# Splitting the convolution's x loads and v stores by partitions: 120 and 8, later 108 and 20, then 88 and 40

## The chip, the core and the metric

The kernel runs on one core of a Trainium2 chip. The metric is the device time of one execution in microseconds; lower is better. A profiled execution also gives the span of the program's instructions, which is a little shorter than the device time, and all positions in time below ("at 207 us") are counted from the start of that span.

## The reference, cut to what matters

Two layers, each of the form x + f(group norm of x), on x of shape 16 images × 16 channels × 256 × 256, float32:

```python
# layer 0: a circular 3x3 convolution, written in the reference with FFTs
x = x + conv3x3_circular(gn(x), L0_conv_weight)
# layer 1: a Laplace neural operator (poles and residues)
x = x + laplace(gn(x), ty, tx, poles1, poles2, residues)

def gn(v, G=8, eps=1e-5):          # per image and group of 2 channels
    ...
    return (g - mean) / sqrt(var + eps)

def laplace(...):
    alpha = fft2(x)                # steady part: alpha times a rational function, back by ifft2
    S = einsum('ikpq,oikp,xikq->oxik', residues, A, Bm)
    x1 = ifft2(einsum('biox,oxik->bkox', alpha, S)).real
    ...                            # transient part: sums over poles of exp(pole * t)
    return x1 + x2 / Nx / Ny
```

The change concerns layer 0 alone: how its input x comes into the on-chip memory and how its result, called v, goes out to DRAM.

## The kernel before, in words

The program has four stages, one after the other: the convolution (29 to 587 us), transforms of v along y and x (to about 1125 us), the mixing of channels (to about 1860 us), and the transforms back with the output. The change is in the first.

**How an image is laid out.** The 128 partitions hold 4 row groups × 2 rows × 16 channels. An image comes as two halves, tiles `xt` of 128 partitions × 18 rows × 258 floats, in a pool of five buffers. `load_x` loads a half in four parts (`PARTS`: rows 0, 4, 10, 14, 18), one DMA each from `load_part` (L132). In DRAM each partition's two neighbouring rows are one piece of 2064 bytes, so a part has 2 or 3 pieces per partition.

**The order of work.** The stage is written out by hand in a loop over `g`, 24 steps per image (L687). Its first call in each step is `conv(g)` (L292): 16 matmuls of 32 × 32 on 512 columns, four row groups side by side (they stand in the profile as 768 matmuls and 768 weight loads of L306 per image). After six steps a quarter of an image's sums is ready: ScalarE copies it out of PSUM into `pair` and `far` (L325). Two steps later `mirror` lets VectorE form the sum of the two halves (L273) and GpSimd the difference (L276). ScalarE squares both for later statistics (L284). Seven and eight steps after the copy, the two `vD<-pair` stores are issued (L335), eight per image; each piece in DRAM is 2048 bytes. `pair` has three buffers, `far` two.

**When x is loaded.** Images 0 and 1 are loaded before the loop. In image b, at steps 4, 5, 10, 11 of each half image, one part of image b + 2 is loaded. Its first reader is VectorE: `x_stats(b)` (L184) takes moments by `bn_stats` (L191), one row pair each, and at fixed steps before the image begins gathers them, spreads them by a matmul (L219), forms the variances (L229 to L239) and at the end the scaled weights `wc` (L249). The convolution of the image can't begin before `wc`.

**Queues.** All these loads and stores are issued by SyncE (SP), in program order. An instruction that waits, a store for GpSimd's difference for instance, holds up those behind it. SP uses eight completion semaphores in turn, and an issue waits until the earlier transfer on its semaphore has landed.

**Beside it.** A generator, `tables`, is advanced once per step and builds tables for the second layer: among others it loads `s_h` in five transfers (L455) at about 62, 129, 203 and 276 us, and stores `cD` in eight (L647) between 385 and 520 us. At the end of the stage the first loads of v for the next stage, `s<-vD` (L746), follow the last stores on SP.

Of the kernel before, what the change touches and what calls it, by code (L numbers as in the profile page):

```python
# [16 lines left out]
B = 16  # L17
C = 16
N = 256
P = 128  # L20
# [4 lines left out]
def conv_then_laplace_kernel(ctx: ExitStack, tc: tile.TileContext, a: dict, out: bass.AP):  # L25
# [15 lines left out]
    nc = tc.nc  # L41
    x = a["x"]
# [29 lines left out]
    vD = []  # L72
    for b in range(B // 4):
        t = dp.tile([P, C, 8 * N + 256], FP, name=f"vD{b}", tag=f"vD{b}")
# [53 lines left out]

    PARTS = 0, 4, 10, 14, 18

    def load_part(t, b, h, i, j):
        nc.sync.dma_start(  # L132
            out=t[:, i:j].rearrange("p (n r) x -> p n (r x)", r=2),
            in_=x[b][:, 8 * h + i // 2 : 8 * h + j // 2, 0 : 2 * (N + 2)],
        )

    def load_x(b, h):
        t = xp.tile([P, 18, N + 2], FP, name="xt", tag="xt")
        for i, j in zip(PARTS, PARTS[1:]):
            load_part(t, b, h, i, j)  # L140
        return t
# [129 lines left out]
    def mirror(g, b, u, pair, hi):  # L271
        both, lo = pair[:, :, :, 0], pair[:, :, :, 1]
        nc.vector.scalar_tensor_tensor(  # L273
            both, lo, 1.0, hi, ALU.mult, ALU.add, accum_out=sums[:, b, u : u + 1]
        )
        nc.gpsimd.tensor_tensor(lo, lo, hi, ALU.subtract)  # L276
        folded.extend((g + 7 + r, b, u, pair, r) for r in range(2))
        squared.append((g + 5, lambda: square(both, 4 + 2 * u, b, bias=shift2[:, b : b + 1])))
        squared.append((g + 7, lambda: square(lo, 5 + 2 * u, b)))
# [12 lines left out]
    def conv(g):  # L292


        for c in range(4):
            for r in range(4):
                at = g if r < 2 else g - 3
                if not 0 <= at < 24 * B:
                    continue
                b, u, n = at // 24, at // 6 % 4, at % 6  # L300
                phase, tap = n // 3, n % 3
                if n == 0 and c == 0:
                    acc[r] = pc.tile([P, 2, N], FP, name="ps_conv", tag="ps_conv")
                q = 8 * (u % 2) + c + phase + (r < 2)
                rows = slice(32 * r, 32 * r + 32)
                nc.tensor.matmul(  # L306
                    acc[r][32 * c : 32 * c + 32],
                    lhsT=ready[b][0][rows, phase, tap],
                    rhs=halves[b][u // 2][rows, q : q + 5 : 4, 2 - tap : 2 - tap + N],
                    start=n == 0,  # L310
                    stop=n == 5,
                )
        for r in (0, 1) if g % 6 == 5 else (2, 3) if g % 6 == 2 else ():
            at = g if r < 2 else g - 3
            if not 0 <= at < 24 * B:
                continue
            b, u = at // 24, at // 6 % 4
            if r == 0:
                pair = vp.tile([P, 2, 2, 2, N], FP, name="pair", tag="pair")
                acc["v", 0] = pair, pair[:, :, :, 1]  # L320
            elif r == 2:
                far = fp.tile([P, 2, 2, N], FP, name="far", tag="far")
                acc["v", 1] = far, far
            to = acc["v", r // 2][1]
            nc.scalar.activation(to[:, r % 2], acc[r], AF.Identity, bias=ready[b][1])  # L325
            if r == 3:
                later.append((g + 2, lambda g=g, b=b, u=u, pair=acc["v", 0][0], hi=to: mirror(g, b, u, pair, hi)))
        while later and (later[0][0] <= g or g >= 24 * B + 2):
            later.pop(0)[1]()
        while squared and (squared[0][0] <= g or g >= 24 * B + 2):  # L330
            squared.pop(0)[1]()
        while folded and (folded[0][0] <= g or g >= 24 * B + 2):
            _, b, u, pair, r = folded.pop(0)
            y = 64 * r + 16 * u
            nc.sync.dma_start(  # L335
                out=vD[b // 4][y : y + 16, :, b % 4].rearrange("(t y) c h x -> (y c) t (h x)", t=2),
                in_=pair[:, r].rearrange("p t h x -> p t (h x)"),
            )

    vs = tp.tile([P, 5, B], FP, name="vs", tag="vs")  # L340
    vrhs = tp.tile([P, 2, B, C], FP, name="vrhs", tag="vrhs")
# [345 lines left out]
    for g in range(24 * B + 3):  # L687
        conv(g)
        if g - 24 * (B - 4) in (16, 19, 22, 27, 30, 33):
            next(early, None)  # L690
        b, n = divmod(g, 24)
        if b + 2 < B and n % 12 in (4, 5, 10, 11):
            h, k = n // 12, (4, 5, 10, 11).index(n % 12)
            if k == 0:
                halves.setdefault(b + 2, []).append(
                    xp.tile([P, 18, N + 2], FP, name="xt", tag="xt")
                )
            load_part(halves[b + 2][h], b + 2, h, PARTS[k], PARTS[k + 1])
        for b, gen in at_step.get(g, ()):
            going.append([b, gen, next(gen)])  # L700
        for it in list(going):
            while it[2] is not None and g >= 24 * it[0] - it[2][0]:
                it[2][1]()
                it[2] = next(it[1], None)
            if it[2] is None:
                going.remove(it)
        run_jobs(g, slots.get(n, ()))
        next(tables, None)
# [32 lines left out]
    m, n = cols[:, 16:17], cols[:, 17:18]  # L741
# [140 lines left out]
    nsgn, first = mcol[:, 7:8], mcol[:, 8:9]  # L882
# [61 lines left out]
    for u in range(len(units) + 1):  # L944
        at = units[u] if u < len(units) else None
        if at is not None:
            now = vq
            t = lp.tile([P, 2, 4, 3, P], FP, name="t", tag="t")
# [8 lines left out]
        if last is not None:  # L957
            i, b0 = last[:2]
# [13 lines left out]
        if last is not None:  # L972
            first_slots(b0, spec, *done)
            if b0 == B - 4:
                project(i, psd)
                (nc.sync if i + 1 < C else nc.scalar).dma_start(
                    out=aD[:, 2 * i : 2 * i + 2], in_=spec.rearrange("p r f b -> p r (f b)")
# [25 lines left out]
    pair = a0.tile([P, 4, 4, 2, 16, B], FP, name="abd01", tag="abd01")  # L1003
# [420 lines left out]
    for n, (k, b0) in enumerate(units):  # L1424
# [13 lines left out]
        r = rp.tile([P, 4, 2, N], FP, name="r", tag="r")  # L1438
# [169 lines left out]
```

## Time and profile before

| | us |
|---|---|
| median of three runs | 2661.2 (2646.39 to 2662.68) |
| profiled execution, device time | 2645.82 |
| profiled execution, span | 2643.7 |
| convolution stage (29 to 587 us of the span) | 558 |
| PE busy in that stage | 507.1 |
| VectorE (DVE) busy in that stage | 409.8 |

In the profile, PE is TensorE's matmuls and PEld its weight loads, DVE is VectorE, ACT ScalarE, POOL GpSimd, and SPq the transfers that SyncE issues. A row of a tile, as `xt<-in_x`, names what is written and what is read. A wait row gives the engine and line that waited, what released it, the total, the number of times and the longest. "issue" stands where the profile shows no releaser. The page's rows with 40 digits cut the span into equal slices of 66 us and give the busy share in tenths; "share of 16 engines" means the 16 DMA engines of the core.

### The profile page before, as it was taken

The page shows a single profiled execution, that of the slowest core. Times are in us where ns is not written, and L with a number is a line of the kernel's source. Part 1 is how long each engine was busy: PE and PEld are TensorE (multiplying, and loading weights), DVE is VectorE, ACT ScalarE, POOL GpSimd, SP SyncE. Part 2 cuts the span into 40 slices and gives each one's busy share as a digit, 9 for nine tenths or more (in the row PEclk, how much of TensorE's full clock was granted, in tenths as well). Part 3 has the DMA queues.
Part 4 walks back from the last instruction along what each step waited for, and adds up shares of the span by engine and source line. Part 5 has one row for each costly group of instructions (what it writes and reads, how often), then busy time and mean ns, then how long its engine had stood idle before and what let it go on. Part 6 is the DMA issues. An engine that isn't in the chain of part 4 may idle for free.

```text
span 2643.7 us, 83901 instructions
## 1 busy us (share of the span) xinstructions
PE 2483.2 (94%) x35314; PEld 1880.4 (71%) x35314; DVE 1983.8 (75%) x3805; ACT 1450.5 (55%) x2727; POOL 1327.4 (50%) x1179
## 2 busy tenths in 40 slices
PE   5988899889999999998999999999799999999998
PEld 2444454466777777775887878888688888888887
DVE  7767778838888888888787878888266676667666
ACT  2555566575666666665666666666244444444443
POOL 1333368432333333334476746676556565665653
PEclk9999999999999999999999999999899999999999
DMA  8787778855465556545777777877988888888884
GB/s 278 267 282 271 268 244 296 287 189 186 192 255 233 193 212 241 224 189 219 225 229 223 229 228 217 236 227 230 257 284 304 286 292 277 295 290 279 294 284 172
DMA packets 313399, 653.11 MB, mean 247 GB/s; under 512 B 44566, under 2 KB 159382, under 8 KB 301120
## 3 DMA queue, kind: packets, MB, share of 16 engines
q1 hardware_dynamic: 311856, 640.55, 71.7%
q8 instruction: 278, 4.55, 0.7%
q0 software_dynamic: 896, 3.02, 0.4%
q10 hardware_dynamic: 272, 4.19, 0.4%
q14 instruction: 97, 0.79, 0.1%
HBM read 368.15 MB, written 280.36 MB: 245 GB/s over the span
## 4 chain that ended last, share of the span: by engine, by line
PE 61%; DMA 5%; DVE 4%; SPq 4%; ACT 2%; issue 1%; POOL 1%; ACTq 0%; DVEq 0%; POOLq 0%
PE ps_mix L1120 9%; PE ps_y L777 9%; PE ps_p L1361 9%; PE ps_y L785 8%; PE ps_f L1385 8%; PE ps_f L1386 8%; PE ps_x L820 5%; DMA yD<-yt 4%; PE ps_s L1032 2%; SPq L1134 2%; PE ps_h L1345 2%; PE psd L805 1%; DVE sg L1052 1%; ACT yt L1233 1%; SPq L1102 1%
## 5 line engine op out<-in xcount | busy, mean ns | idle before, releaser
L1120 PEld LDWEIGHTS ps_mix<-abd,sg 128*64 128x64 f32 x8192 | 450.6, 138 | 85.9 <-ACT yt L1233 54.1
L1120 PE MATMUL ps_mix<-abd,sg 128*64 128x128 f32 x8192 | 480.7, 276 | 32.5 <-DMA yD<-yt 17.7
L306 PE MATMUL ps_conv<-xt,wc 32*32 32x512 f32 x12288 | 453.5, 618 | 45.2 <-issue 37.2
L1325 POOL TENSOR_TENSOR u<-yk 128x512 f32<-128x512 f32 (+1 forms) x268 | 352.3, 1347 | 282.8 <-PE ps_p L1361 215.5
L306 PEld LDWEIGHTS ps_conv<-xt,wc 32*32 32x32 f32 x12288 | 254.7, 104 | 231.9 <-issue 147.7
L793 ACT ACTIVATE t<-ps_y,vmr 128x384 f32<-128x384 f32 x512 | 297.5, 581 | 162.6 <-PE ps_y L785 162.5
L1052 DVE STREAM_SHUFFLE sg<-ps_s 128x512 f32<-128x512 f32 (+1 forms) x264 | 329.3, 1316 | 0.0
L777 PE MATMUL ps_y<-tabE,vq 128*128 128x256 f32 x1024 | 313.1, 388 | 13.4 <-DVE vq L766 11.7
L276 POOL TENSOR_TENSOR pair<-pair,far 128x1024 f32<-128x1024 f32 x64 | 151.8, 2372 | 332.9 <-DVE pair L273 277.5
L785 PE MATMUL ps_y<-tabO,vq 128*128 128x256 f32 x1024 | 305.6, 380 | 0.0
L1385 PE MATMUL ps_f<-pt,inv 128*128 128x256 f32 x1008 | 300.4, 380 | 0.0
L1361 PEld LDWEIGHTS ps_p<-inv,u 128*128 128x128 f32 x2048 | 266.2, 193 | 47.3 <-issue 25.5
L1386 PE MATMUL ps_f<-hs,ey 128*128 128x256 f32 x1008 | 299.8, 379 | 0.0
L1389 DVE TENSOR_TENSOR r<-ps_f,q 128x256 f32<-128x256 f32 x256 | 107.1, 418 | 252.7 <-ACT q L1388 252.7
L1361 PE MATMUL ps_p<-inv,u 128*128 128x128 f32 x2048 | 279.3, 280 | 10.5 <-POOL u L1329 10.4
L1049 ACT ACTIVATE sg<-ps_s,mcol 128x512 f32<-128x512 f32 (+1 forms) x264 | 179.5, 690 | 184.4 <-DVE sg L1052 117.0
L777 PEld LDWEIGHTS ps_y<-tabE,vq 128*128 128x128 f32 x1024 | 189.3, 190 | 90.2 <-ACT q L833 50.3
L1388 ACT COPY q<-ps_f 128x256 f32<-128x256 f32 x256 | 95.4, 373 | 288.1 <-PE ps_f L1386 285.4
L765 POOL TENSOR_TENSOR vq<-vf 128x512 f32<-128x512 f32 x64 | 81.5, 1274 | 294.5 <-DVE vf L769 277.6
L1363 ACT COPY pt<-ps_p 128x512 f32<-128x512 f32 x256 | 150.2, 587 | 132.6 <-PE ps_p L1361 128.0
L1233 ACT COPY yt<-ps_mix 128x512 f32<-128x512 f32 x352 | 185.1, 592 | 55.3 <-DMA yD<-yt 43.3
L785 PEld LDWEIGHTS ps_y<-tabO,vq 128*128 128x128 f32 x1024 | 195.4, 191 | 26.8
(239 smaller groups left out, 4050.8 us busy)
## 6 DMA issues: line engine op xcount, KB each, us to landing
vD<-pair SPq DMA_DIRECT2D x128, 512.0 KB
yD<-yt SPq DMA_DIRECT2D x512, 128.0 KB
vl<-vD SPq DMA_DIRECT2D x128, 512.0 KB
out_y<-ol SPq DMA_DIRECT2D x128, 512.0 KB
s<-vD SPq DMA_DIRECT2D x126, 512.0 KB
aD<-spec SPq DMA_DIRECT2D x15, 4096.0 KB
yk<-yD SPq DMA_DIRECT2D x60, 1024.0 KB
xt<-in_x SPq DMA_DIRECT2D x96, 516.0 KB
```

The source lines that it names most:

```text
L306: nc.tensor.matmul(acc[r][32 * c : 32 * c + 32], lhsT=ready[b][0][rows, phase, tap], rhs=halves[b][u // 2][rows, q : q + 5 : 4, 2 - tap : ...
L777: nc.tensor.matmul(ps[:, 0:N], lhsT=vf[:, xo, 0, j], rhs=tabE[:, 0 : i + 2 : i + 1], start=True, stop=False, skip_group_check=True,)
L785: nc.tensor.matmul(ps[:, P : P + N], lhsT=vf[:, xo, 1, j], rhs=tabO[:, i : C + 1 : C - i], start=False, stop=True, skip_group_check=True,)
L793: nc.scalar.activation(t[:, xo, j].rearrange("p l n -> p (l n)"), ps[:, 0:384], AF.Copy, scale=vmr[:, 0, b0 + j, i : i + 1],)
L1049: nc.scalar.activation(to[..., k : k + 2], src[odd], AF.Copy, scale=nsgn)
L1052: nc.vector.stream_shuffle(to[..., C + k : C + k + 2], src[1 - odd], swap)
L1120: nc.tensor.matmul(ps[64 * t : 64 * t + 64, j], lhsT=sg[:, f : f + 2].rearrange("p f m -> p (f m)"), rhs=abd[jq][:, :, 2 * t + cc, 2 * jj ...
L1233: (nc.vector.tensor_copy if m >= (2 if late else 3) else nc.scalar.copy)(o, src)
L1325: nc.gpsimd.tensor_tensor(u[:, :, j].rearrange("p b (c n) -> p c b n", c=8), in0, in1, o)
L1361: nc.tensor.matmul(ps[:, at], lhsT=u[:, n], rhs=tab, start=True, stop=True)
L1385: nc.tensor.matmul(ps[:, e], lhsT=tab, rhs=pt[:, e], start=True, stop=False)
L1386: nc.tensor.matmul(ps[:, e], lhsT=ey[:, e], rhs=hs, start=False, stop=True)
```

## The change

A helper gives a cut of the 128 partitions for an image number: 120 for images below 6, 108 below 11, 88 from there on. Each part of x from image 2 on is loaded by two DMAs, one for the partitions below the cut and one for the rest. Each store of v is likewise two DMAs, with the cut of the image that is being loaded at the time (two ahead, at most 15). What is transferred, the tiles and all other instructions stay as they are.

```diff
+    def spans(b):
+
+        first = 120 if b < 6 else 108 if b < 11 else 88
+        return (0, first), (first, P)
+
     def load_part(t, b, h, i, j):
-        nc.sync.dma_start(
-            out=t[:, i:j].rearrange("p (n r) x -> p n (r x)", r=2),
-            in_=x[b][:, 8 * h + i // 2 : 8 * h + j // 2, 0 : 2 * (N + 2)],
-        )
+        for p, q in spans(b) if b > 1 else ((0, P),):
+            nc.sync.dma_start(
+                out=t[p:q, i:j].rearrange("p (n r) x -> p n (r x)", r=2),
+                in_=x[b][p:q, 8 * h + i // 2 : 8 * h + j // 2, 0 : 2 * (N + 2)],
+            )
...
             y = 64 * r + 16 * u
-            nc.sync.dma_start(
-                out=vD[b // 4][y : y + 16, :, b % 4].rearrange("(t y) c h x -> (y c) t (h x)", t=2),
-                in_=pair[:, r].rearrange("p t h x -> p t (h x)"),
-            )
+            to = vD[b // 4][y : y + 16, :, b % 4].rearrange("(t y) c h x -> (y c) t (h x)", t=2)
+            for p, q in spans(min(b + 2, B - 1)):
+                nc.sync.dma_start(out=to[p:q], in_=pair[p:q, r].rearrange("p t h x -> p t (h x)"))
```

## The prediction

> **What bounds the kernel now.** I read the page first, then the convolution by windows of one image (cut at every 768th matmul of L306, which is an image's worth), its waits, and the order of time around one image boundary, each with its lines here.
>
> ```profile
> DMA  8787778855465556545777777877988888888884
> ...
> q1 hardware_dynamic: 311856, 640.55, 71.7%
> ...
> vD<-pair SPq DMA_DIRECT2D x128, 512.0 KB
> ...
> xt<-in_x SPq DMA_DIRECT2D x96, 516.0 KB
> ```
>
> ```profile
> 387.80:422.30 34.50, 32.21 (x851) 17.23 (x845) 29.99 (x53) 23.82 (x47) 32.34 (x34) 1.00 0.92 316
> 422.30:457.80 35.50, 33.06 (x848) 17.71 (x838) 30.57 (x54) 22.62 (x45) 27.86 (x30) 0.95 0.78 271
> ...
> 535.00:560.90 25.90, 25.90 (x780) 18.15 (x785) 16.17 (x38) 17.51 (x33) 8.34 (x4) 1.00 0.45 166
> 560.90:586.80 25.90, 25.90 (x788) 19.21 (x761) 4.93 (x8) 20.16 (x34) 10.89 (x6) 1.00 0.46 166
> ```
>
> The convolution is the first eight and a half slices (29 to 587 us), and DMA is busy there at 7 to 8 tenths, nearly all of it on SP's queue q1 and most of it with stores of v and loads of x. In the windows the columns are length, busy time of PE, PEld, DVE, ACT, POOL, clock, DMA share and GB/s. Images 10 and 11 take 34.5 and 35.5 us at a DMA share of 0.92 and 0.78; images 14 and 15, with no x left to load, take 25.9 us at 0.45, with PE never idle. So PE sets the pace, but something in the images with loads costs it time.
>
> The waits of 33 to 590 us (total, times, longest), then the timelines of SP, DVE and PE around image 6:
>
> ```profile
> POOL pair L276 <- DVE pair L273: 275.3, 48, 47.3
> ...
> PE ps_conv L306 <- issue: 37.2, 26, 5.0
> ...
> DVE xst L191 <- DMA xt<-in_x: 16.4, 5, 5.4
> ```
>
> ```profile
> SPq L335 <- POOL pair L276: 202.8, 44, 8.5
> ...
> SPq L132 <- DMA s_h<-hD: 6.6, 6, 1.7
> ```
>
> ```profile
> 206.14 1.47 SPq L335 DMA_DIRECT2D vD<-pair  x2
> 207.66 1.81 SPq L132 DMA_DIRECT2D xt<-in_x  x2
> ```
>
> ```profile
> 218.25 2.61 DVE L191 BATCH_NORM_STATS2 xst<-xt 128x6 f32<-128x512 f32 x4 [4.75 <-DMA xt<-in_x]
> ...
> 242.15 0.42 DVE L249 SCALAR_TENSOR_TENSOR wc<-wband,xq,imask 128x192 f32<-128x192 f32 x1
> ```
>
> ```profile
> 242.67 2.02 PE L306 MATMUL ps_conv<-xt,wc 32*32 32x512 f32 x32 [4.18 <-issue]
> ```
>
> This is how a late transfer reaches PE. Parts of x issued at 207.7 land at 218.2; DVE waits 4.75 us for them; its chain of statistics ends with wc (L249) at 242.57, and PE, idle 4.18 us with no releaser named, starts image 6 at 242.67. POOL's long wait for DVE is the other face of it: POOL and the stores that follow it hang on DVE's order. The same happens before images 4 and 8 (2.9 and 5.0 us): together 12 of the 37.2 us. The other 25 us are 23 gaps of at most 2.4 us, most of which end about 2.3 us after a 16 KB packet of the instruction queue (q8) began. There are 99 such packets in the stage, median 0.97 us, and none of these gaps in images 14 and 15, where DMA is light.
>
> [...] xt and vD transfers raise their semaphore 16 times, s_h (slowest dimension 8) 9 times[...] and the 8-partition yk transfers 9 times. So 120 and 8 give 15 and 8 engines, 108 and 20 give 12 and 10, 88 and 40 give 11 and 10. [...]
>
> **The change, part by part.** First the load of one engine. In a backlog (transfers landing from 145 to 157 us) completions follow each other by 1.2 us for a vD store (16 packets per engine), 1.3 for a part of x with 16 packets, 2.0 for one with 24: about 78 ns a packet. An image has 8 stores, 6 small and 2 large parts: 9.8 + 7.8 + 4.0 = 21.6 us on every engine. Split by 120 and 8, engines 0 to 7 carry 9 partitions for 8 and engine 15 none: 24.3 us. By 108 and 20, engines 0 to 9 carry 11: 29.7 us. By 88 and 40 they carry 12: 32.4 us.
>
> *Images 0 to 3* (x of 2 to 5, v of 0 to 3). A burst of two stores and two parts is 72 packets, 5.7 us; it becomes 6.4. From landing to first use by L191 most parts have 4 to 9 us left, so it is hidden, except behind s_h: its five transfers of 1.75 us put 8.7 us on engines 0 to 7 alone, and around 74 and 145 us the parts have no slack. Two events, 1 us each: +2 us.
>
> *Images 4 to 8* (x of 6 to 10, v of 4 to 8). The burst takes 7.8 us, 2.1 more. Behind s_h at 203 and 276 us that is +2.5 us each on DVE, and with no work to hide it, on PE at the boundary; the other parts hide it in their slack, except two at 360 us with 1.7 and 3.3 us: +1. Sum +6 us.
>
> *Images 9 to 13* (x of 11 to 15, v of 9 to 13). The 32.4 us are joined by the stores of cD (32 packets per engine of 47 ns, two per image: 3.2 us) and the engine's share of the instruction packets (99 × 0.97 us over 16 engines and 16 images: 0.4 us): 36.0 us of work on ten engines. The five images now take 180 us (355.1 to 535.0), 36.0 each. So DMA would have to run without a pause, and it can't: SP waits in order for POOL's subtraction before a store (202.8 us in the stage), x stands behind it, and the eight completion semaphores that SP uses in turn (100 to 107 in the trace) now cover four old transfers instead of eight. I take a tenth of pauses, 40 us an image: +20 us. The lower bound is +3 (no pauses). The upper one follows from the only row for fewer than 16 engines, s_h, whose 16 packets take 1.75 us (109 ns, not 78): 32.4 becomes 45.3, with the rest 48.9 us, +65 in these five images.
>
> *Issuing.* 112 more parts and 128 more stores at 0.45 us (vD in the trace 0.37 to 0.42, x 0.38 to 1.3): SP's 12 us an image become some 19 of 36. The second of a pair waits for nothing that the first hadn't; each burst's end moves by up to 1.8 us, inside the slack and counted in the tenth above: 0. At the end, the first s load stands on SP behind two stores (586.6 and 587.1) and DVE waits for it while PE is idle 11.7 us: two more issues and a longer store, +1.5 us.
>
> *Instruction packets.* Where they go decides this term. After a q8 packet one engine's completion comes about 1 us later, and in the backlogs behind s_h, where engines 0 to 7 run late as a group, the late one is now in that group (packets at 70.7, 76.6, 213.1, 219.2), now in the other (142.5, 148.7, 225.2, 284.5). So they move around, and the total DMA work doesn't change: a packet finds a free engine more often (1, 4 or 5 of 16), but a deeper queue otherwise. I take 0, with -20 and +15 as ends.
>
> Sum: 2 + 6 + 20 + 1.5 = 29.5, rounded 30 us. The profiled execution took 2645.8 us (span 2643.7), the median of the three runs is 2661.2; I add to the median: 2691 us.
>
> **Rivals.**
>
> *Instruction packets win* (0.19): the freed engines are those that the instruction packets mostly use. For it: 25 us of PE gaps, none where DMA is light. Against: late engines in both groups. With the 25 us gone and 5 lost to full engines, 2641 us; this is the one on the other side. It decides once more than half of the gaps go and images 9 to 13 stay within 37 us.
>
> *All is hidden* (0.17): DMA in images 9 to 13 fills its pauses, or a 120-partition transfer is still dealt over all engines, so that only the issues are added. For it: 36.0 us fit 36.0. Against: no pause at all is needed. +8: 2669 us.
>
> *Fewer engines are slower each* (0.22): s_h's 109 ns hold for every split. The engine loads become 34.0, 41.6 and 45.3 us. Images 0 to 3 still fit: +2. Images 4 to 8 (171.9 to 355.1 us, 36.6 each) need 41.6 + 0.4 + 3.5 (two events of s_h over five images) = 45.5: +44. Images 9 to 13: +65. With the end, +112: 2773 us. For it: packets of s_h reach 157 ns, twice the common 84. Against: its 8 engines all read the same 16 rows, which x and v don't.
>
> **How the numbers follow.** Forecast 0.42, with its own range 2679 to 2716; rivals 0.19, 0.17, 0.22. The range for 8 in 10 goes from 2640, which leaves out half of the first rival, to 2775, which leaves out the upper half of the third. About 1% (27 us) is what a measurement of this kernel can tell from no change. Slower by more: 0.30 of the forecast's 0.42 and the 0.22 of the third rival, 0.52. Faster by more: 0.07, the better end of the first rival. The rest, 0.41, is within 1%.
>
> **What would show it.** Right: images 9 to 13 at 38 to 42 us with a DMA share near what it was (the same work, on fewer engines); DVE's wait for xt in the stage well above 16.4 us; PE's boundary gaps at images 6 and 8 longer by 2 to 3 us; semaphores of the large transfers raised 15, 12 and 11 times plus one. Images 14 and 15 stay at 25.9 us and everything after 600 us only shifts. The forecast is wrong if the "issue" gaps of PE fall below some 20 us, if packets of 2 KB take over 100 ns in the mean, or if the stage ends within 5 us of 587.

## The result, and the profile after

The changed kernel takes 2686.86 us in the median of three runs (2686.58 to 2695.14), against 2661.2 before: a ratio of 1.0128, with a 95% interval of 1.0098 to 1.0158, or 26 to 42 us. The two medians are 25.7 us apart, at the low end of that interval; three runs of each, which range over 16 and 9 us, don't tell the size better. The forecast was 2691.

The two profiled executions differ by more, 49.3 us (2695.14 against 2645.82), since the one before ran 15.4 us under the median of before and the one after 8.3 us over its own. Of the 49.3 us, 34.6 lie in the convolution, whose last matmul ends at 621.9 us for 587.3. The other 15 lie in later stages, in lines that the change doesn't touch; these stages range over some 20 us between the profiles of the kernels below, which are equal there. They are not read as an effect.

The page of the kernel after, in the parts shown of before (tenths of DMA busy in slices of 67 us, SP's queue, shares of the chain that ended last) and the group of the convolution's matmuls:

```profile
DMA  8887777765555665565777777777978888888884
...
q1 hardware_dynamic: 313264, 640.56, 71.5%
...
PE 69%; DMA 17%; DVE 5%; SPq 3%; issue 3%; ACT 1%; POOL 1%; DVEq 0%; ACTq 0%; POOLq 0%
...
L312 PE MATMUL ps_conv<-xt,wc 32*32 32x512 f32 x12288 | 459.7, 619 | 53.1 <-issue 40.4
```

Bytes are the same and packets nearly so. A matmul took as long in the mean of the stage (619 ns; 618 before). DMA holds 17% of the chain, against 5% before; in the line list beside it, `xt<-in_x` alone has 9%. The windows by group of images say where the time went. First before, then after; the rows are images 0 to 3 (cut 120 after), 4 to 8 (108), 9 to 13 (88), 14 and 15, each from the first matmul of its first image (the stage's last 48 matmuls, 3.2 us, lie behind the last row), and the columns are those of the prediction's windows:

```profile
29.30:169.40 140.10, 124.36 (x3053) 66.40 (x3055) 108.11 (x249) 75.54 (x130) 43.35 (x22) 0.97 0.79 271
169.40:353.50 184.10, 168.19 (x3899) 88.70 (x3902) 124.00 (x263) 103.59 (x178) 57.45 (x28) 0.95 0.75 259
353.50:532.30 178.80, 160.58 (x4137) 85.44 (x4112) 155.01 (x293) 110.61 (x216) 124.02 (x124) 0.98 0.83 286
532.30:584.10 51.80, 51.09 (x1557) 36.21 (x1535) 22.30 (x50) 37.67 (x65) 19.00 (x8) 1.00 0.47 170
```

```profile
29.30:178.30 149.00, 125.89 (x3055) 64.52 (x3059) 108.05 (x249) 74.66 (x129) 43.22 (x22) 0.98 0.87 253
178.30:365.80 187.50, 167.69 (x3898) 86.22 (x3904) 124.39 (x263) 104.63 (x180) 57.35 (x28) 0.97 0.77 255
365.80:565.20 199.40, 169.02 (x4137) 88.04 (x4123) 146.45 (x292) 109.53 (x216) 121.00 (x125) 0.93 0.73 248
565.20:618.70 53.50, 51.19 (x1553) 36.00 (x1531) 23.29 (x47) 37.67 (x65) 18.77 (x8) 1.00 0.60 191
```

The groups grow by 8.9, 3.4, 20.6 and 1.7 us. In images 9 to 13 the DMA share falls from 0.83 to 0.73, but share times length is the same (0.83 × 178.8 = 148 us, 0.73 × 199.4 = 146): the same work, with more pauses. In images 0 to 3 it is not (0.79 × 140.1 = 111, 0.87 × 149.0 = 130): the engines are busy 19 us longer for the same bytes.

What PE waited for in the convolution, before (33 to 576 us) and then after (33 to 610 us), as total, times and longest. The rows with "issue", for which the profile shows no releaser, are called PE's unnamed gaps from here on:

```profile
PE ps_conv L306 <- issue: 37.2, 26, 5.0
PE ps_stat L219 <- DVE xe L212: 4.2, 3, 1.8
PE ps_conv L306 <- ACT pair L325: 3.5, 3, 2.2
PE ps_setup L631 <- DVE vmr L389: 3.1, 1, 3.1
PE ps_stat L361 <- DVE vs L355: 1.5, 1, 1.5
```

```profile
PE ps_conv L312 <- issue: 40.4, 32, 3.9
PE ps_stat L225 <- DVE xe L218: 14.8, 8, 3.9
PE ps_conv L312 <- ACT pair L331: 7.7, 4, 3.5
PE ps_setup L636 <- DVE vmr L394: 5.7, 1, 5.7
PE ps_stat L366 <- DVE vs L360: 4.2, 1, 4.2
```

These waits grow from 49.5 to 72.8 us, by 23.3; PE's busy time in the same stretches grows by 9.0 (492.45 to 501.43). Images 9 to 13, where the granted clock was 0.93 for 0.98, have 8.4 us more; the other groups have a little more or less. The largest growth, 10.6 us, is a matmul of the statistics (L225) that waits for DVE. What DVE, ACT and POOL waited for in that stage after:

```profile
POOL pair L282 <- DVE pair L279: 273.2, 44, 47.3
...
DVE xst L197 <- DMA xt<-in_x: 71.9, 40, 6.8
...
ACT pair L331 <- DMA vD<-pair: 50.7, 18, 4.8
```

DVE's wait for x was 16.4 us in 5 waits and is 71.9 in 40. ACT's copy into `pair`, whose buffer a store must leave first, waits 50.7 us. And SP's own waits in images 9 to 13, first of the kernel after, then (one line) of the kernel before:

```profile
SPq L138 <- DMA xt<-in_x: 40.7, 44, 2.4
SPq L343 <- DMA vD<-pair: 19.7, 31, 1.4
...
SPq L343 <- POOL pair L282: 3.7, 2, 3.0
```

```profile
SPq L335 <- POOL pair L276: 51.8, 13, 8.5
```

Before, SP waited for GpSimd's difference, for ScalarE's part of cD (42.3 us), and for landings of x and v under 1 us in all. After, it waits for landings, 75 times for 60.4 us in these two rows, since each of its eight semaphores comes round twice as soon and the landings are late (for all 256 stores of v after, the next issue on the same semaphore began only after the last raise; the cut by pieces below shows that the sooner turn alone doesn't do it); GpSimd is no longer late, SP is. Image 12 of the kernel after shows the path, in the timelines of SP, DVE, ACT and PE (start, length, instruction, in brackets the idle time before it and its releaser):

```profile
482.81 5.73 SPq L138 DMA_DIRECT2D xt<-in_x  x4
488.64 4.39 SPq L343 DMA_DIRECT2D vD<-pair  x4
```

```profile
494.48 1.29 DVE L197 BATCH_NORM_STATS2 xst<-xt 128x6 f32<-128x512 f32 x2 [4.63 <-DMA xt<-in_x]
```

```profile
500.29 1.27 ACT L331 ACTIVATE pair<-ps_conv,xq 128x512 f32<-128x512 f32 x2 [4.75 <-DMA vD<-pair]
```

```profile
514.66 0.60 PE L366 MATMUL ps_stat<-vs,g 128*128 128x12 f32 x2 [4.19 <-DVE vs L360]
```

Four loads take SP 5.7 us and four stores 4.4. DVE then waits 4.6 us for x, ACT 4.8 for a store, and PE 4.2 for a result of DVE, which comes late in turn.

The trace tells on how many engines a transfer runs. Counted in it, the parts of x and v of 120, 8, 108, 20, 88 and 40 partitions raise their semaphores 16, 9, 13, 11, 12 and 11 times. One of these raises comes early, at the median about 0.5 us after the issue begins; in a whole transfer of x or v, 16 raises, none comes before 2.5 us. Less the early one they are 15, 8, 12, 10, 11 and 10, the numbers of engines that the forecast took; the trace of before doesn't show them for these cuts. The packets agree: most often 16 are in flight at once in images 0 to 3, 4 to 8 and 9 to 13 before, and 15, 12 and 11 after. So the two transfers of a pair share engines, as the forecast took it; which engine a packet ran on isn't in the trace.

The mean duration of a packet of x (2064 bytes) in images 0 to 3, 4 to 8 and 9 to 13 was 93, 94 and 96 ns before and is 126, 107 and 101 ns after. Packets of 2048 bytes, which are v (and in the first two groups some of s_h), went from 94, 95 and 93 to 96, 90 and 90 ns; v is read from on-chip memory instead of written to it. So in these images the loads slow and the stores don't, most where the cut is 120. Only in images 14 and 15, where no x is loaded beside it, does a packet of v take longer, 102 ns for 88. The experiments start from that.

### The profile page after: what moved, and what is told of

It is laid out like the page before. It is cut to its first block, busy times and chain, and to the rows that moved or that the text cites. A ratio compares the mean times of both kernels' runs of the same rounds, so it can differ in the third digit from the quotient of the medians.

```text
span 2693.4 us, 84487 instructions
## 1 busy us (share of the span) xinstructions
PE 2499.3 (93%) x35314; PEld 1884.0 (70%) x35314; DVE 1983.2 (74%) x3805; ACT 1450.3 (54%) x2727; POOL 1323.8 (49%) x1179
## 4 chain that ended last, share of the span: by engine, by line
PE 69%; DMA 17%; DVE 5%; SPq 3%; issue 3%; ACT 1%; POOL 1%; DVEq 0%; ACTq 0%; POOLq 0%
PE ps_mix L1125 12%; PE ps_y L782 9%; DMA xt<-in_x 9%; PE ps_p L1366 8%; PE ps_y L790 8%; PE ps_f L1390 8%; PE ps_f L1391 8%; PE ps_x L825 4%; PE ps_conv L312 4%; PE ps_s L1037 3%; DMA yD<-yt 3%; DMA vD<-pair 3%; PE ps_h L1350 2%; PE psd L810 1%; SPq L1139 1%
## 5 line engine op out<-in xcount | busy, mean ns | idle before, releaser
L312 PE MATMUL ps_conv<-xt,wc 32*32 32x512 f32 x12288 | 459.7, 619 | 53.1 <-issue 40.4
L782 PE MATMUL ps_y<-tabE,vq 128*128 128x256 f32 x1024 | 313.5, 388 | 12.3 <-DVE vq L771 10.8
L782 PEld LDWEIGHTS ps_y<-tabE,vq 128*128 128x128 f32 x1024 | 189.7, 191 | 88.8 <-ACT q L838 50.3
L197 DVE BATCH_NORM_STATS2 xst<-xt 128x6 f32<-128x512 f32 x256 | 164.4, 682 | 77.0 <-DMA xt<-in_x 76.8
```

Source lines behind the costliest of these rows:

```text
L312: nc.tensor.matmul(acc[r][32 * c : 32 * c + 32], lhsT=ready[b][0][rows, phase, tap], rhs=halves[b][u // 2][rows, q : q + 5 : 4, 2 - tap : ...
L782: nc.tensor.matmul(ps[:, 0:N], lhsT=vf[:, xo, 0, j], rhs=tabE[:, 0 : i + 2 : i + 1], start=True, stop=False, skip_group_check=True,)
```

## The experiments

The theory on trial was that of the forecast: uneven load on the engines, felt only where DMA has no slack. Its rivals were the number of transfers, and slower packets in every load of x that is cut by partitions, at any load of the engines.

Each edit is against the kernel before. `spans` below stands for the change's helper; where only its line is shown, `load_part` and the store of v use it as in the change. Ratios are to the kernel before, run on the same chip, whose median was 2656.8 to 2658.4 us in these three sets; a ratio of 1.001 is 2.7 us.

### Two transfers, cut by pieces

```diff
     def load_part(t, b, h, i, j):
+        for i, j in ((i, i + 2), (i + 2, j)) if b > 1 else ((i, j),):
...
+            for t in range(2):
+                nc.sync.dma_start(out=to[:, t], in_=pair[:, r, t].rearrange("p h x -> p (h x)"))
```

> Every part of x from image 2 on and every store of v is two transfers, as in the change, but cut by pieces of a row and not by partitions: each half still covers all 128 partitions, so all 16 engines carry the same. The number of transfers, of issues and of semaphore turns is that of the change. Engine load theory (the forecast): the number alone costs 0 to 5 us. Rival (issues and the eight semaphores that now cover half the bytes are what costs): most of the change's 26 us, 18 us or more, with the wait of DVE for xt near the changed kernel's 71.9 us.

Ratio 0.9986 (0.9971 to 1.0001). The same number of transfers, issues and semaphore uses as in the change, each with all 128 partitions, costs nothing. In images 9 to 13 of this kernel, with SP's own wait for x last:

```profile
PE ps_conv L307 <- issue: 7.5, 8, 1.8
...
DVE xst L192 <- DMA xt<-in_x: 0.7, 1, 0.7
```

```profile
SPq L133 <- DMA xt<-in_x: 1.4, 2, 1.0
```

DVE hardly waits for x, and SP waited 1.4 us where it waits 40.7 in the kernel after. Waiting for landings on SP's semaphores needs slow landings too; the number of issues alone doesn't cause it. The rival of issues falls. Packets of x took 100 ns here in all three groups, so a mean near 100 ns is no sign of a price by itself.

### One cut at a time

```diff
+        return ((0, 120), (120, P)) if b < 6 else ((0, P),)
```
```diff
+        return ((0, 108), (108, P)) if 5 < b < 11 else ((0, P),)
```
```diff
+        return ((0, 88), (88, P)) if b > 10 else ((0, P),)
```

> Only images below 6 by the cut are split (120 and 8), all others whole. Forecast: +2 us, since 9/8 of the load hides in the slack. Rival ([...]in the changed kernel a 2064-byte packet of x took 126 ns in images 0 to 3, against 93 before): +6 to +12 us, packets of x again near 126 ns in images 0 to 3 and 93 later.

> Only images 6 to 10 by the cut are split (108 and 20). Forecast: +6 us, by 2.5 us at each of the two image boundaries behind s_h. Rival (slower packets, 107 ns there in the changed kernel): +8 to +15 us over these images. If only the late split matters: 0 to 3 us.

> Only images from 11 on by the cut are split (88 and 40). Forecast: +20 us, images 9 to 13 at about 40 us each, packets of x not above 105 ns, because ten engines carry 12 partitions for 8. If the cost were spread evenly over the split images (issues), it would be about 11 us.

| cut alone | ratio (95%) | its images: before, whole change, alone, us | x packet there |
|---|---|---|---|
| 120 | 1.0036 (1.0021 to 1.0051) | 140.1, 149.0, 148.9 | 125 ns |
| 108 | 1.0029 (1.0012 to 1.0046) | 184.1, 187.5, 189.7 | 102 ns |
| 88 | 1.0076 (1.0054 to 1.0098) | 178.8, 199.4, 195.4 | 99 ns |

Times 2656.8, these are 9.6, 7.7 and 20.2 us. They add up to 1.0141, within the interval of the whole, so nothing shows that the parts hide each other. Of the price of 88 alone, 16.6 us lie in its images; images 14 and 15, which still store v in two parts, took 59.0 us for 51.8 in its profile. The cut at 120 costs 9.6 us where 2 were forecast. Late x alone doesn't account for it. In images 0 to 3 before, with 120 alone, and after the whole change:

```profile
PE ps_conv L306 <- issue: 11.5, 9, 2.9
...
DVE xst L191 <- DMA xt<-in_x: 6.0, 2, 4.4
```

```profile
PE ps_conv L311 <- issue: 16.4, 10, 2.3
...
DVE xst L196 <- DMA xt<-in_x: 8.0, 2, 4.5
```

```profile
PE ps_conv L312 <- issue: 20.7, 14, 2.6
...
DVE xst L197 <- DMA xt<-in_x: 11.3, 3, 6.8
```

DVE's wait for x grows by 2.0 us with 120 alone, PE's unnamed gaps by 4.9 (PE is also busy 3.2 us longer, at a clock of 0.95 for 0.97); in the whole the gaps grow by 9.2. Counted in the trace over all of PE's matmuls, those unnamed gaps that end 1.7 to 3.2 us after a packet of the instruction queue began go from 7.9 us to 15.7 and 21.2 there. Such stretches cover a quarter of the time, so chance would put a quarter of the gaps there, and nearly all lie there. In the kernels below whose images 0 to 3 are loaded whole, the same count is 8 to 12 us. In images 9 to 13 the other path rules, DVE late on x. The kernel with 88 alone:

```profile
DVE xst L196 <- DMA xt<-in_x: 29.9, 16, 3.7
ACT pair L330 <- DMA vD<-pair: 29.0, 10, 4.4
...
PE ps_conv L311 <- issue: 11.4, 8, 3.1
```

### Even load, still cut by partitions

Each count above, 16 for a whole transfer and 15, 12, 11, 10, 10 and 8 for 120, 108, 88, 40, 20 and 8 partitions, is the largest number up to 16 that divides the partitions. From this, and with equal shares for the engines of a transfer, the author estimated the loads of the cuts below, for which no count was taken: 112 and 16 partitions give 16 engines 7 and 1 each, 96 and 32 give 6 and 2, eight per engine, as before; 104 and 24 load some engines with 10. The rival is again that of slower packets of x.

```diff
+        return ((0, 112), (112, P)) if b < 6 else ((0, P),)
```
```diff
+        return ((0, 96), (96, P)) if b > 10 else ((0, P),)
```
```diff
+        return ((0, 104), (104, P)) if b > 10 else ((0, P),)
```

> Images below 6 by the cut are split at 112: 112 and 16 rows run on 16 engines each, 7 and 1 partitions, so the load stays even (8 per engine)[...]. Forecast's theory (uneven load alone costs): 0 to 2 us, packets of x near 95 ns in images 0 to 3. Rival[...]: packets of x well above 100 ns, and +5 to +10 us, as with 120 and 8, which cost 9.6 us at 125 ns.

> Images from 11 on by the cut are split at 96: 96 and 32 rows run on 16 engines each, 6 and 2 partitions, an even load. Forecast's theory: the 20 us of the 88 and 40 split vanish, 0 to 4 us are left, images 9 to 13 at some 36 us each. Rival (splitting itself late in the stage, where cD's stores are also on SP): 10 us or more remain.

> Images from 11 on by the cut are split at 104: 13 engines with 8 partitions and 12 engines with 2, so twelve engines carry 10 for 8 and three none. By the forecast's sum that is 27 us of x and v and 3.6 of other work for images of 36 us: it fits, so 0 to 5 us of the 20. If the cost grew in proportion to the excess load, it would be half, 10 us.

| cut alone | most partitions of one engine (estimated) | ratio (95%) | x packet there |
|---|---|---|---|
| 112, early | 8 | 1.0026 (1.0013 to 1.0039) | 127 ns |
| 96, late | 8 | 1.0076 (1.0050 to 1.0103) | 127 ns |
| 104, late | 10 | 1.0070 (1.0046 to 1.0095) | 112 ns |
| 88, late | 12 | 1.0076 (1.0054 to 1.0098) | 99 ns |

112 costs 7 us with a load that is even by the estimate, and its interval overlaps that of 120. Late in the stage, loads of 8, 10 and 12 cost the same. By the estimate load alone is therefore not the cause, and the expected 0 to 4 us for 96 and 0 to 5 for 104 failed. But equal prices here are not one path. In images 9 to 13 with 96:

```profile
PE ps_conv L311 <- issue: 20.2, 15, 3.0
...
DVE xst L196 <- DMA xt<-in_x: 4.8, 6, 1.9
```

Beside the lines for 88 above, the even cut has x in time (4.8 us of waits against 29.9) and PE's unnamed gaps doubled (20.2 us, 10.9 before); the count of gaps after instruction packets doubles alike, from 11.7 to 22.5 (4 to 14 us in the kernels whose x isn't cut at 96 there). The uneven cut has the gaps as before and x late. 104 is in between (13.0 and 7.1 us). And the packets of x are hardly slowed at 88, whose 99 ns are those of the cut by pieces, nor at 108 (102 ns).

### Which of the two directions

The cut 96 in the load of x alone, then in the store of v alone; the other direction stays whole.

```diff
+        return ((0, 96), (96, P)) if b > 10 else ((0, P),)
...
+        for p, q in spans(b) if b > 1 else ((0, P),):
```
```diff
+        return ((0, 96), (96, P)) if b > 10 else ((0, P),)
...
+            for p, q in spans(min(b + 2, B - 1)):
```

> Images from 11 on by the cut: x alone is split at 96 and 32, v is stored whole. If slow packets of x (127 ns with both split) are the cause of that kernel's 20 us: 14 to 20 us, with PE's gaps after instruction packets in images 9 to 13 near 22 us as there, against some 10 in kernels without that split. If the number of transfers late in the stage is the cause: about half, 10 us.

> The counterpart: v alone is split at 96 and 32, x is loaded whole. Packets of v stayed at 94 ns with both split. If slow packets of x are the cause: 0 to 4 us. If the number of transfers is: about 10 us.

x alone: 1.0055 (1.0037 to 1.0073), 14.6 us, packets of x at 123 ns. v alone: 1.0014 (1.0001 to 1.0027), 3.7 us, packets of x at 101 and of v at 98 ns. PE's unnamed gaps in images 9 to 13, with x alone and with v alone:

```profile
PE ps_conv L311 <- issue: 17.8, 14, 2.4
```

```profile
PE ps_conv L311 <- issue: 12.1, 13, 2.3
```

Most of the price belongs to the loads of x. The stores aren't free of it: in images 14 and 15, with no x beside them, packets of v took 102 to 111 ns in the kernels that cut v at 88, 96 or 104, and 88 to 89 where v is whole.

### The cuts by themselves

At the start of the kernel the halves of images 0 and 1 are loaded with little beside them; each half is cut in its own way. The first numbers of the expectation are those of load alone, the second those of the rival, slower packets; the loads at 64 and 96 are estimated as above.

```diff
+        cut = {(0, 0): 120, (0, 1): 64, (1, 0): 88, (1, 1): 96}.get((b, h))
+        for p, q in ((0, cut), (cut, P)) if cut else ((0, P),):
```

> The loads of images 0 and 1 alone, at the start, where no store runs beside them: the first half of image 0 is cut at 120, its second half at 64, the first half of image 1 at 88, its second at 96; whole halves take 6.2 us of landing in the kernel before. The most loaded engine has 81, 72, 108 and 72 packets of 2064 bytes. If only that load counts (84 ns a packet, as in whole transfers): 6.8, 6.1, 9.1 and 6.1 us. [...] packets of 120 ns and more, 9 to 11 us for 120, 10 to 12 for 64, 9 for 96, and about 10 for 88, which has eleven engines only.

| a half (1152 packets) | first to last packet, us | packet, ns | load alone would give, us (estimated from the row of whole) |
|---|---|---|---|
| whole | 6.3 to 6.7 | 88 to 94 | |
| 120 and 8 | 11.2 | 156 | 6.3 × 9 / 8 = 7.1 |
| 64 and 64 | 12.5 | 169 | 6.3 |
| 88 and 40 | 12.9 | 156 | 6.3 × 12 / 8 = 9.5 |
| 96 and 32 | 12.9 | 148 | 6.3 |

The last two rows are less clean than the rows of 120 and 64: they are the halves of one image, and engines that are done with the first go on to the second (they end their shares of it between 37.7 and 50.3 us, see below). Together they took 26.0 us for 13.3 whole.

Windows of the start, whole first, then with the cuts 120 and 64 (the last columns are DMA share and GB/s):

```profile
6.00:12.00 6.00, 0.00 (x0) 0.00 (x0) 4.25 (x7) 0.00 (x0) 0.00 (x0) 1.00 1.05 396
```

```profile
6.00:12.00 6.00, 0.00 (x0) 0.00 (x0) 2.30 (x4) 0.00 (x0) 0.00 (x0) 1.00 1.03 210
12.00:18.00 6.00, 0.00 (x0) 0.00 (x0) 2.58 (x4) 0.00 (x0) 0.00 (x0) 1.00 1.08 193
```

The engines are as busy and move half as much. This is the slowing by itself, for even and uneven cuts alike: each of the four takes 1.7 to 2 times as long as a whole load, at 64, 88 and 96 longer even than the 9 to 12 us that the rival expected. (The run was made for these loads; the kernel's time is of one execution and isn't compared.)

The slowing is measured, its cause is not. Which partitions an engine takes isn't in the trace; the semaphores give only the number of engines. And a packet of x is a read from DRAM and a write on the chip: no run tells a slow read from a slow write.

The uneven load is seen here as well, by the raises of the semaphores: after the half cut at 88, five engines end their share of the next transfer at 37.7 to 38.0 us, one at 43.5 and ten at 48.9 to 50.3.

### The transfers on eight engines, spread over sixteen

The forecast laid the late x before images 6 and 8 on `s_h`, whose five loads run on eight engines: each raises its semaphore 9 times, once early (1.0 to 1.1 us after the issue begins), and at 131.0 to 132.8 us before, where they run alone, the DMA share is 0.53, most often with eight packets in flight. All 16 rows that it reads are copies of the first (the kernel makes them itself), so it can as well read eight rows 16 times.

```diff
-                    in_=hD[j, side, :, at].unsqueeze(0).to_broadcast([8, 16, n]),
+                    in_=hD[j, side, 0:8, at].unsqueeze(0).to_broadcast([16, 8, n]),
```

> Nothing is split. The five loads of s_h (four times) take 8 of their 16 equal source rows and repeat them 16 times instead of 16 rows 8 times, so that they run on 16 engines and not on 8; the values are the same. By the forecast's reading of the kernel before, the late parts of x behind s_h (DVE waits 16.4 us, PE 12 us at three boundaries) are due to the load of engines 0 to 7: DVE's wait for xt should fall below 5 us and the kernel become faster by 5 to 12 us. If those waits have another cause, 0.

Ratio 0.9969 (0.9957 to 0.9982), 8 us faster. Its semaphores count 16 for each of these loads, where they counted 9 before. In the stage:

```profile
PE ps_conv L306 <- issue: 32.7, 26, 3.6
...
DVE xst L191 <- DMA xt<-in_x: 5.2, 6, 1.4
```

DVE's wait for x falls from 16.4 to 5.2 us, and images 4 to 8 from 184.1 to 174.8. The reading of these boundaries in the forecast holds.

### Both together

This one and the cut by pieces, in one kernel.

> The two changes that lost nothing, together: s_h on 16 engines (0.31% faster alone) and x and v in two transfers by pieces (0.14% faster alone, its interval just touching no change). If they add up: 0.4 to 0.5% faster than the kernel before, about 11 us. If they shorten the same waits: 0.3%.

2636.56 us, ratio 0.9923 (0.9897 to 0.9948): faster than both kernels. The two ratios multiply to 0.9955, so they add at least; that it gained more than the 0.4 to 0.5% expected isn't explained, and that they help each other isn't shown. In its stage PE's unnamed gaps are 26.7 us, and DVE's wait for x is 1.0; before they were 37.2 and 16.4, with the cut by pieces alone 33.9 and 14.6.

## Why the prediction was right, and where its terms were not

The direction and the sum were right: 30 us forecast, 26 to 42 measured, 34.6 in the stage of the profile. The terms were not all.

*Images 9 to 13: +20 forecast, +20.6 in the profile, +20.2 with 88 alone.* Right in size, and in signs: 39.9 us an image (38 to 42 were named), the same DMA work, DVE's wait for x far above 16.4 us, SP held by its eight semaphores. The size owes something to luck: the sum has two stores of cD an image where the kernel has eight in the five images (the 3.2 us should be 2.4), and the tenth of pauses was a guess; with 2.4 it would have given some 16 us. The reason was half of it. Uneven load does go with late x and v here (DVE's wait for x is 29.9 us with 88 alone, ACT's for a store 29.0), but the cut at 96, even by the estimate, costs as much, by the other path (4.8 us of waits for x). Of the 20.6 us, 8.4 are PE busy at a clock of 0.93; whether the change lowers the clock is not settled, since other kernels of the study had 0.98 in the same images at the same price.

*Images 0 to 3: +2 forecast, +9.6 with 120 alone, +8.9 in the profile.* This is the term that failed. It was made of engine loads at 78 ns a packet. The forecast took nothing for slower packets of any cause. Packets of x took 126 ns (93 before). What came was what the third rival named, slower packets, though not for its reason, fewer engines: the cut at 112, by the estimate even and over sixteen engines, has 127 ns and costs 7 us. The rival gave +2 for these images as well, since it counted the slack of the landings and not the gaps of PE.

*Images 4 to 8: +6 forecast, +7.7 with 108 alone, +3.4 in the whole.* The size was right within the intervals, the place was not. The gaps at the start of images 6 and 8, 4.2 and 5.0 us, became 1.7 and 3.5, not 2 to 3 us longer. The late x was paid 19 us earlier, at the statistics matmul of the same image:

```profile
233.91 0.70 PE L225 MATMUL ps_stat<-xe,ones 128*128 128x256 f32 x2 [3.88 <-DVE xe L218]
...
309.28 0.89 PE L225 MATMUL ps_stat<-xe,ones 128*128 128x256 f32 x2 [2.89 <-DVE xe L218]
```

Before, these two waits were nothing and 1.2 us. Both gaps of a boundary taken together grew by 1.4 us at image 6 (3.88 + 1.7 against 4.2) and by 0.2 at image 8 (2.89 + 3.5 against 1.2 + 5.0).

*Issuing: 0.* Right, by the cut by pieces.

*End of the stage: +1.5 forecast; the gap went from 11.7 to 10.8 us.* It didn't come. Images 14 and 15, forecast to stay as they were, took 1.7 us more.

*Instruction packets: 0 forecast.* Over the stage the count after instruction packets is 25.2 us before and 36.0 after. That isn't a clear difference: it is 23.5 in the kernel cut by pieces, but 34 with s_h on sixteen engines, which is faster, and 36 with v alone cut at 96. By groups it is clear where the loads became slow (images 0 to 3, +13.3, against 8 to 12 us in the kernels that load them whole). Where engines came free (images 9 to 13) it shrank from 11.7 to 6.4, but the cut by pieces, with all 128 partitions in each transfer, has 4.8 there. So the first rival, which bet on the free engines, isn't shown to have gained anything. Why slow loads should lengthen these gaps isn't shown: on which engine each instruction packet ran, and what it waited for there, isn't in the trace.

*The rivals.* "All is hidden" falls with images 9 to 13. "Fewer engines are slower each" gave +65 there and +44 in images 4 to 8 by 109 ns for everything; x reached 101 and 107 ns, v 90, and images 4 to 8 grew by 3.4 us, not 44. The forecast's own sign for being wrong, packets of 2 KB over 100 ns in the mean, came in (x and v together 101.2 ns), and it points at the right step, the loads. By the profile the total held in part by luck: 6.9 us too few in images 0 to 3 stood against 2.6 too many in images 4 to 8 and 2.4 at the end of the stage.

*Open.* A packet of x cut at 88 takes 156 ns at the start but 101 in the loop, and one cut at 96 148 and 127. Stores run beside the loads in the loop and not at the start; no run shows what that does to either, and it wouldn't tell the two cuts apart. How much of the 20 us at the cut 88 is load and how much slower loads can't be told from these runs, as no run has the load of 88 without a cut by partitions; that its packets are no slower than those of the cut by pieces (99 and 100 ns) speaks for the load.

## What to carry to other kernels

Before a load to on-chip memory is cut by partitions, time the cut load by itself, with nothing beside it, and don't count only the packets per engine: a cut by pieces, which leaves all 128 partitions in each transfer, cost nothing here, and every cut of x by partitions cost something. A late transfer was paid here at L225 (3.88 us at image 6), 19 us before the boundary where it was forecast, so look for it at every matmul that hangs on the chain and not only at the boundary where it was seen before. And look for broadcasts with a small slowest dimension: s_h, with 8, raised its semaphores 9 times, once early; with 16 it raised them 16 times, and that was worth 8 us.

## What the runs showed of the hardware that was not expected

- Loads cut at 120 or 64 partitions ran at 193 to 222 GB/s where whole ones ran at 396, with the engines equally busy; an image cut at 88 and 96 took 26.0 us for 13.3. Packets grew from 88 to 94 ns to 148 to 169 ns. Stores from on-chip memory grew far less: 90 to 98 ns beside loads of x, and 102 to 111 ns for 88 where no x was loaded.
- PE's gaps that follow packets of the instruction queue were 12 us in images 9 to 13 before and 21 to 23 us with x cut at 96, though x came in time for DVE (4.8 us of waits or less): slow loads went with idle PE even where no instruction is seen to wait for them.
